# A cross-interaction (CIN) kernel: all products in tiles of 32 rows by 64 columns, without joined leftovers

## The chip, the core and the metric

The kernel runs on one core of one Trainium2 chip. The metric is the device time of one execution in microseconds (us); the figure of the kernel before is the median of three runs. The engines are called PE (TensorE, the matrix unit), PEld (its weight loads), DVE (VectorE), ACT (ScalarE), POOL (GpSimd) and SP (SyncE).

## What is computed

`x` holds 1024 batches of 39 fields with 64 elements each. Three layers each combine the last result with the fields, a different weight for every pair; the sums over the elements go through one final row of weights. All is float32.

```python
def _cin_layer(Xk, X0, W, b):
    Wr = W.reshape(O, Hk, Fdim)
    return jnp.einsum('bhe,bfe,ohf->boe', Xk, X0, Wr) + b[None, :, None]
X0 = sparse_embedding            # (1024, 39, 64)
Xk = X0
for W, b in ((W0, b0), (W1, b1), (W2, b2)):      # 64 outputs each
    Xk = _cin_layer(Xk, X0, W, b)
    outs.append(Xk.sum(axis=-1))
return jnp.concatenate(outs, axis=-1) @ fc_w.T + fc_b
```

## The kernel before

**The algebra.** Both kernels use the same one. The third layer's outputs are only ever summed with weights, so its weights are folded with those of the final row into one matrix `v2`, and that into the weights of layer 2. What is left are two bilinear forms of the fields with 64 outputs each: one is the first layer, the other the folded rest. For each batch and element the two results are multiplied with each other and summed over the elements. A bilinear form is a weighted sum over pairs of fields, and x_a x_b is x_b x_a, so 780 products, each with the sum of two weights, and 39 linear terms (a product with a row of ones) do for both forms. The table of all weights, one row for each output of both forms, is `both`.

**Products and matmuls.** A column is one batch and element, and a block `n` is 2048 columns (32 batches), so there are 32 blocks. GpSimd gathers five operand tiles of 128 rows by 2048 columns for a block (`roll`, L178, an indirect DMA each, L174) from a DRAM table `xd` in which every field is a row; the row numbers stand in `lists`. Six products of two such tiles (`PAIRS`, `product`, L213 and L219, on DVE) hold nearly all pairs. Each is multiplied with its weights `wa` (`multiply`, L555): four matmuls of 128 rows by 128 columns by 512 (L559), the 128 outputs being both forms. A block has 24 such matmuls.

**The leftover.** 32 rows of pairs and 32 of linear terms do not fill a tile. They are done for two blocks at once, with four row tiles of 32: `u` and `v` are gathered as 128 rows by 1024 (`roll_small`, L183), multiplied (L221), and `join` (L567) runs 16 matmuls of 32 rows by 64 columns (L579) and 8 linear ones (L590) into the eight banks of the two blocks.

**Order.** The program is written out in order by hand. `steps` lists the products; DVE makes each four steps ahead (`AHEAD`), into one of four buffers `p`. `finish` (L613) reads a block's four PSUM banks: ACT adds a bias to one form (`z`, L607), DVE multiplies it with the other (`g`, L609) and sums over elements (L620); `fields` (L598) adds the 39 field rows as further rows of `g`. The eight PSUM banks hold two blocks. The operand tiles have two buffers, `rt[0]` and `rt[1]`: when the last product of block `n` is issued, POOL is given the gathers of block `n+2`. The tables `xd` are loaded one block at a time, later by SP.

**Start and end.** `x`'s first two quarters come by ACT's queue into half tables `xh` and are gathered from there. Weights are folded by matmuls (L406 to L487), put into `both` (last copy L503), summed to pairs for one product at a time (`weight_rows`, L515, on DVE at L526), turned by PE (`weight_turn`, L536, L543) and copied to `wa` by ACT (L544). The first three products are made in pieces, and the other weights are turned between the first matmuls. At the end the last block is finished one bank at a time (`finish_quarter`, L627, sums at L631), then `last_weights` (L638) turns the folded row to a column (L640, L649), and a few short matmuls (L745, L757) make the output.

Of the kernel before, what the change touches and what calls it, by code (L numbers as in the profile page):

```python
# [1 line left out]

# [14 lines left out]
NG = 3  # L64
K = NG * F
NX = 128 - K
NT = 5
STEP = (0, 2, 2, 3, 1)
BASE = (0, 35, 11, 1, 17)
OFFSET = (0, 1, 3, 2, -1)  # L70
ONLY = 9
PAIRS = ((0, 1), (0, 2), (3, 1), (3, 2), (0, 4), (3, 4))
NPAIR = len(PAIRS)
SQUARE = 32
NCHUNK = NPAIR + 2
MM = 512
SUB = 1024
BLK = 2048
NA = 10
NQ = NA // 2  # L80
NW = 3
NF = F // NW
BB = BLK // E
SB = SUB // E
NBLK = B // BB
NTAB = 3
# [3 lines left out]
U_STEPS = ((10, -29), (20, -8), (23, -2), (25, -36), (28, 32))  # L90
V_STEPS = ((0, -3), (20, 6), (25, 33), (28, -35), (31, -39))


def label(i, row):
    if row < K:
        return (row % F + BASE[i] + STEP[i] * (row // F)) % F
    e = row - K
    if i == NT - 1 and e < ONLY:
        return F
    return 3 * e + (e >= ONLY) + (e > ONLY) + OFFSET[i]  # L100


def small_labels(r):
    u = 4 + r + 2 * min(r, 23) + sum(by for at, by in U_STEPS if r >= at)
    return u, u + sum(by for at, by in V_STEPS if r >= at)


def split(labels, taken):

    rows = []  # L110
    for row, ab in enumerate(labels):
        key = tuple(sorted(ab))
        if key not in taken:
            taken.add(key)
            rows.append((row, *ab))
    runs = []
    while rows:
        n = 1
        if len(rows) > 1:
            by = [y - x for x, y in zip(rows[0], rows[1])]  # L120
            kind = (rows[0][1] == rows[0][2], rows[0][2] == F)
            while (
                n < len(rows)
                and by[0] == 1
                and by[1] > 0
                and by[2] == (0 if kind[1] else by[1])
                and [y - x for x, y in zip(rows[n - 1], rows[n])] == by
                and (rows[n][1] == rows[n][2], rows[n][2] == F) == kind
            ):
                n += 1  # L130
        row, p, q = rows[0]
        runs.append((row, n, p, q, by[1] if n > 1 else 1, by[2] if n > 1 else 1))
        rows = rows[n:]
    return runs


_taken = set()
RUNS = [
    split([(label(i, row), label(k, row)) for row in range(128)], _taken) for i, k in PAIRS
]  # L140
RUNS.append(split([small_labels(r) for r in range(SQUARE)], _taken))
RUNS.append(split([(small_labels(r)[0], F) for r in range(SQUARE)], _taken))
assert _taken == {(a, b) for a in range(F) for b in range(a, FT)}
assert max(2 * s + b for s, b in zip(STEP, BASE)) <= F
# [3 lines left out]
def cin_kernel(ctx: ExitStack, tc: tile.TileContext, x, w0t, b0, w1, b1, w2, b2, fc_w, fc_b, out):  # L148
# [6 lines left out]
    prods = ctx.enter_context(tc.tile_pool(name="prods", bufs=4))  # L155
    psum = ctx.enter_context(tc.tile_pool(name="psum", bufs=8, space=PSUM))
# [3 lines left out]
    xd = [dram.tile([2 * FT, BLK], F32, name=f"xd{k}") for k in range(NTAB)]  # L160
    xh = [dram.tile([F, SUB], F32, name=f"xh{k}") for k in range(2)]

    def bank(name):
        return psum.tile([128, MM], F32, name=name, tag="po")

    def load(n, engine=nc.sync):
        first = n % 2 * FT
        engine.dma_start(  # L168
            xd[n // 2 % NTAB][first : first + F].rearrange("f (b e) -> f b e", e=E),
            xv[:, n * BB : (n + 1) * BB, :],  # L170
        )
# [53 lines left out]
    with prep as prep:  # L225
# [222 lines left out]
        for k in range(7):  # L448
            turn_w0(k)
# [356 lines left out]
```

## Time and profile before

| what | value |
|---|---|
| time, median of 3 runs | 733.13 us (733.05 to 733.62) |
| span of the profiled execution | 731.4 us |
| matmul and weight-load records, each | 2375 |
| granted TensorE clock (row PEclk) | 9 in all 40 slices, 90% of full speed or more |
| data moved by DMA | 197.24 MB, 270 GB/s on average |
| packets of the gathers' queue (q0) | 65.5% of 16 engines' span |

The profile is one execution. Its span runs from the first to the last instruction; the measured time has a little on top of it. "Busy" is the time in which an engine works on an instruction. A row of the groups gives busy time and the mean of one in ns, then the idle time ahead of the group and what ended it. Rows of a timeline or of the chain begin with the start in us and the duration. `r` stands for the operand tiles, `p` for products, `po` for the banks of sums.

### The profile page before, as it was taken

Reading aid. Unit: us, or ns where it says so; the run is one execution under the profiler, and the core shown is the slowest. Engines: PE = TensorE matmul, PEld = TensorE weight load, DVE = VectorE, ACT = ScalarE, POOL = GpSimd, SP = SyncE. Lnnn points to the kernel's source line nnn. Section 1 sums busy time; section 2 is a strip of 40 time slices with the busy share of each in tenths; the row PEclk is TensorE's granted clock in tenths of the full one; section 3 lists DMA queues with packets and bytes.
Section 4 is the critical chain, followed back from the end, with each engine's and each line's share of the span. In section 5 each row is a group of like instructions: output and inputs, shape, how many; then the busy total and the mean of one; then the engine's idle time right before and its main releaser. Section 6 shows DMA issues by size and latency. Waiting matters only on the chain.

```text
span 731.4 us, 6351 instructions
## 1 busy us (share of the span) xinstructions
PE 724.7 (99%) x2375; PEld 316.1 (43%) x2375; DVE 638.3 (87%) x521; ACT 166.9 (23%) x240; POOL 397.6 (54%) x254
## 2 busy tenths in 40 slices
PE   8999999999999999999999999999999999999998
PEld 4444444444444444444444444444444444444443
DVE  6999798988889988889988889888898988889885
ACT  3332121222212222221222212222121221212222
POOL 6789886536555445754537555455654547545300
PEclk9999999999999999999999999999999999999999
DMA  8997899789575887757679675896767777565700
GB/s 268 376 337 280 315 342 356 290 307 338 232 273 231 281 336 286 270 225 285 269 288 330 223 289 219 304 348 236 268 256 274 301 287 266 224 252 236 288 0 0
DMA packets 65983, 197.24 MB, mean 270 GB/s; under 512 B 40110, under 2 KB 40179, under 8 KB 45984
## 3 DMA queue, kind: packets, MB, share of 16 engines
q0 software_dynamic: 28784, 185.56, 65.5%
q1 hardware_dynamic: 35468, 9.29, 5.5%
q10 hardware_dynamic: 1700, 1.99, 1.0%
q8 instruction: 18, 0.29, 0.1%
q14 instruction: 13, 0.11, 0.0%
HBM read 196.76 MB, written 10.60 MB: 284 GB/s over the span
## 4 chain that ended last, share of the span: by engine, by line
PE 99%; DVE 0%; DMA 0%; issue 0%; ACT 0%; DVEq 0%
PE po L559 91%; PE po L579 4%; PE po L590 2%; PE idle L279 0%; PE pv L406 0%; PE pt L487 0%; PE small L323 0%; PE pv L487 0%; PE pw L418 0%; DMA fcrow<-in_fc_w 0%; PE tr L543 0%; DVE g L609 0%; DVE pairs L526 0%; DVE sums L631 0%; ACT z L607 0%
## 5 line engine op out<-in xcount | busy, mean ns | idle before, releaser
L559 PE MATMUL po<-p,wa 128*128 128x512 f32 x1536 | 666.0, 594 | 0.0
L219 DVE TENSOR_TENSOR p<-r 128x2048 f32<-128x2048 f32 (+2 forms) x198 | 434.1, 2224 | 72.4 <-PE po L559 67.1
L559 PEld LDWEIGHTS po<-p,wa 128*128 128x128 f32 x1536 | 290.5, 190 | 371.7 <-issue 354.6
L174 POOL DMA_INDIRECT r<-xd,lists x156 | 302.3, 1938 | 267.1 <-issue 266.2
L607 ACT ACTIVATE z<-po,columns 64x512 f32<-64x512 f32 x128 | 87.3, 682 | 380.1 <-PE po L590 217.9
L609 DVE SCALAR_TENSOR_TENSOR g<-po,b0s,z 64x512 f32<-64x512 f32 x128 | 95.9, 749 | 9.3 <-ACT z L607 5.3
L602 ACT COPY g<-r 39x1024 f32<-39x1024 f32 x64 | 66.7, 1043 | 155.0 <-DVE sums L620 126.8
L620 DVE TENSOR_REDUCE sums<-g 103x16 f32<-103x1024 f32 x62 | 75.6, 1220 | 2.1
L174 POOL DMA_INDIRECT u<-xd,lists x16 | 38.9, 2432 | 7.5 <-issue 4.6
L174 POOL DMA_INDIRECT v<-xd,lists x16 | 38.5, 2403 | 4.9 <-issue 4.9
L579 PE MATMUL po<-p,wa 32*64 32x512 f32 x512 | 31.6, 600 | 0.0
L221 DVE TENSOR_TENSOR p<-u,v 128x1024 f32<-128x1024 f32 x16 | 19.5, 1218 | 0.0
L579 PEld LDWEIGHTS po<-p,wa 32*64 32x64 f32 x512 | 9.4, 131 | 20.2 <-issue 19.4
L590 PE MATMUL po<-u,wa 32*64 32x512 f32 x256 | 17.0, 587 | 0.0
L174 POOL DMA_INDIRECT r<-xh,lists x8 | 8.0, 996 | 4.8 <-DVE tmp L387 2.7
L590 PEld LDWEIGHTS po<-u,wa 32*64 32x64 f32 x256 | 5.7, 132 | 8.0 <-issue 8.0
L526 DVE TENSOR_TENSOR pairs<-both 128x2 f32<-128x2 f32 (+27 forms) x59 | 6.1, 171 | 0.2
L544 ACT COPY wa<-tr 128x128 f32<-128x128 f32 x8 | 2.1, 266 | 16.2 <-PE tr L543 16.2
L279 PE MATMUL idle<-const-float32-1.0 128*128 128x256 f32 (+1 forms) x8 | 4.0, 596 | 0.8 <-PEq L793 0.8
L543 PE MATMUL tr<-unit,pairs 128*128 128x128 f32 x8 | 2.4, 294 | 2.2 <-DVE pairs L526 2.2
L543 PEld LDWEIGHTS tr<-unit,pairs 128*128 128x128 f32 x8 | 1.2, 151 | 4.7 <-ACT pairs L524 2.7
L168 POOL DMA_DIRECT2D xd<-in_x x3 | 3.2, 1055 | 0.0
(97 smaller groups left out, 56.7 us busy)
## 6 DMA issues: line engine op xcount, KB each, us to landing
xd<-in_x SPq DMA_DIRECT2D x28, 312.0 KB
r<-xd,lists POOLq DMA_INDIRECT x156, 8.9
xd<-in_x POOLq DMA_DIRECT2D x3, 312.0 KB, 7.6
w2s<-in_w ACTq DMA_DIRECT2D x1, 624.0 KB
w1s<-in_w ACTq DMA_DIRECT2D x1, 624.0 KB
w0s<-in_w0t ACTq DMA_DIRECT2D x1, 380.2 KB
xh<-in_x ACTq DMA_DIRECT2D x2, 156.0 KB
xd<-xh SPq DMA_DIRECT2D x2, 156.0 KB
```

The costliest lines, as they stand in the source:

```text
L174: nc.gpsimd.indirect_dma_start(dst, None, table, bass.IndirectOffsetOnAxis(ap=lists[:, k : k + 1], axis=0))
L219: nc.vector.tensor_tensor(p[:, cols], r[:, i, cols], r[:, k, cols], ALU.mult)
L221: nc.vector.tensor_tensor(p[:, 0:SUB], ut[n // 2 % 2], vt[n // 2 % 2], ALU.mult)
L279: nc.tensor.matmul(idle[:, 0:cols], nc.const_aps.tensor(1.0, (128, 128), F32), nc.const_aps.tensor(1.0, (128, cols), F32), start=True, sto ...
L526: nc.vector.tensor_tensor(out, diagonal(a, b, sa, sb), diagonal(b, a, sb, sa), ALU.add)
L559: nc.tensor.matmul(po[n][m], wa[:, c, side : side + 2 * H], p[:, bass.ts(m, MM)], start=n % 2 == 0 and c == 0, stop=n % 2 == 1 and c == NP ...
L579: nc.tensor.matmul(dst[half * H : half * H + H], wa[rows, NPAIR, at : at + H], p[rows, bass.ts(side, MM)], start=t >= 2, stop=t < 2 and ha ...
L590: nc.tensor.matmul(dst[half : half + H], wa[rows, NPAIR + 1, H : 2 * H], ut[n // 2 % 2][rows, bass.ts(side, MM)], start=False, stop=t < 2,)
L602: nc.scalar.copy(gt[H : H + F], rt[n % 2][0:F, 0, bass.ts(m, SUB)])
L607: nc.scalar.activation(z[one], po[n][m][other], AF.Identity, bias=fc0s[other])
L609: return lambda: nc.vector.scalar_tensor_tensor(g[n][m // 2][0:H, at], po[n][m][one], b0s[one], z[one], ALU.add, ALU.mult)
L620: nc.vector.tensor_reduce(sums[:, b_at : b_at + SB], g[n][m // 2].rearrange("p (b e) -> p b e", e=E), AX.X, ALU.add,)
```

## The change

The division of the work is new; the arithmetic in total is not.

**Layout.** The array is always used as four row tiles of 32 rows, and each row tile has its own columns. A super block is 4096 columns (64 batches): row tile `r` of an operand tile holds 1024 of them. A block is 512 of these per row tile, again 2048 columns in all; there are 33 blocks, since the last is cut into two of 256 per row tile. An operand tile ("slot") is 32 fields for each row tile, and there are 14: eight are the fields in turn from a start (`SHIFT`), one is `LEFT` and five are for the remaining seven fields. All are gathered as 128 rows by 1024 columns from the table seen as (field, row tile) rows. The first 4096 columns are gathered in two halves of 512 (`roll_half`), each from a half table `xh` of 32 batches.

**Products.** One slot times five others is one DVE instruction with five results of 512 columns (`product`, L131, L137), so 25 products are five instructions a block. They go into a ring of four such groups. Each product is multiplied in 32x64 matmuls (L471): two forms times four row tiles, each row tile into its own bank (`po`, four banks, two buffers). The two forms go to the two column halves of the array and alternate between blocks. The linear term needs no product: one more set of four matmuls reads slot 1 itself. Nothing is left over, and `join`, `u` and `v` are gone.

**Weights.** `main_pairs` makes the sums for twenty of the products at once; `repeat` copies them to the four row tiles. Twelve chunks are turned (L438) before the first product's matmul, fourteen after eight units (`LAST_TURNS`), a unit being the eight small matmuls of one product. Scratch space of the weights now lies in `rt[1]`, so the gathers of the second super block come after that point.

**Finish and end.** Two banks are finished together: per block two ACT passes, two products and two sums on DVE, and eight field copies on ACT. The last sums are made for 512 columns of two banks. `last_weights` begins with two DVE copies to `kw`.

GpSimd's queue from the first gathers on, before; `xh_71` and `xh_72` are the half tables, `xd_68` the first table, `r_84` and `r_85` the two buffers of operand tiles, `ones` the row of ones:

```order
L369 DMA xd_68<-ones 16x2x128
L174 DMA r_84<-xh_71,lists 128x1024 x4
L174 DMA r_84<-xh_72,lists 128x1024 x2
L168 DMA xd_68<-in_x 1248x1x64
L174 DMA r_84<-xh_72,lists 128x1024 x2
L174 DMA r_84<-xd_68,lists 128x2048
L174 DMA u_86<-xd_68,lists 128x1024
L174 DMA v_88<-xd_68,lists 128x1024
L174 DMA r_85<-xd_68,lists 128x2048 x5
L477 DMA b0s<-in_b 64x1 x2
```

The same place after; `r_82` and `r_83` are now the two buffers of slots, `xh_68` and `xh_69` the half tables, `xd_66` the table of the second super block:

```order
L265 DMA xh_68<-ones 16x128
L81 DMA r_82<-xh_68,lists 128x512 x14
L265 DMA xh_69<-ones 16x128
L75 DMA xd_66<-in_x 2496x1x64
L265 DMA xd_66<-ones 16x256
L81 DMA r_82<-xh_69,lists 128x512 x14
L345 DMA b0s<-in_b 64x1 x2
L346 DMA b1s<-in_b 128x1x1
L347 DMA b2s<-in_b 64x1
L348 DMA fcb<-in_fc_b 96x1
L265 DMA xd_67<-ones 16x256
L265 DMA xd_65<-ones 16x256
```

Before, eleven gathers fill the first 2048 columns and their leftover and five the next block. Now 14 gathers fill the first 2048 columns and 14 the next, and behind the seven smaller DMAs at the end of these rows 14 follow for the next 4096.

DVE's queue where the first products are made, before; `p` is a product, `pairs` the weight sums:

```order
L219 TENSOR_TENSOR p<-r_84 128x512
L526 TENSOR_TENSOR pairs<-both 128x28
L526 TENSOR_TENSOR pairs<-both 128x11
L526 TENSOR_TENSOR pairs<-both 128x26
L526 TENSOR_TENSOR pairs<-both 128x13
L526 TENSOR_TENSOR pairs<-both 128x24
L526 TENSOR_TENSOR pairs<-both 128x15
L526 TENSOR_TENSOR pairs<-both 128x9
L526 TENSOR_TENSOR pairs<-both 128x2
L219 TENSOR_TENSOR p<-r_84 128x512 x3
```

And after; `ring` is the ring of products, and the weight sums now lie in `r_83`:

```order
L431 COPY r_83<-r_83 128x5x96
L137 TENSOR_TENSOR ring<-r_82 128x512 x5
L137 TENSOR_TENSOR ring<-r_82 128x1024
L137 TENSOR_TENSOR ring<-r_82 128x1536
L390 TENSOR_TENSOR r_83<-r_83 128x21
L390 TENSOR_TENSOR r_83<-r_83 128x28 x4
L431 COPY r_83<-r_83 128x6x96
L137 TENSOR_TENSOR ring<-r_82 128x1024
L137 TENSOR_TENSOR ring<-r_82 128x1536
L137 TENSOR_TENSOR ring<-r_82 128x1024
L137 TENSOR_TENSOR ring<-r_82 128x1536
L137 TENSOR_TENSOR ring<-r_82 128x2560 x5
```

Weight sums stood between single products; now five products and a group of five, in two pieces, come first, then five sums and a copy, and after them products in a row. The diff, cut to its core:

```diff
-NT = 5
...
-PAIRS = ((0, 1), (0, 2), (3, 1), (3, 2), (0, 4), (3, 4))
-NPAIR = len(PAIRS)
-SQUARE = 32
...
+NR = 4
+Q = 128 // NR
...
-SUB = 1024
-BLK = 2048
+SUB = 2 * MM
+BLK = NR * MM
+SUP = NR * SUB
+BB = BLK // E
+SB = SUP // E
+MB = MM // E
+NSUP = B // SB
+NTAB = 3
...
+NB = 5
+SHIFT = (3, 7, 11, 15, 19, 0, 1, 2)
+BACK = (5, 6, 7, 0)
+REST = F - Q
+LEFT = len(SHIFT)
+RIGHT = LEFT + 1
+NSLOT = RIGHT + NB
+NPROD = NB * NB
+LINEAR = NPROD
+NCHUNK = NPROD + 1
+DIRECT = 1
+GROUPS = (3, 0, 1, 2, 4)
+ORDER = [NB * k + j for k in GROUPS for j in range(NB)]
+RING = 4
+PB = FT + NR - 1
+LOW, HIGH = 5, 4
+SPLIT = Q - 1
+BLOCKS = [(s, lo, MM) for s in range(NSUP) for lo in (0, MM)]
+BLOCKS[-1:] = [(NSUP - 1, lo, MM // 2) for lo in (MM, MM + MM // 2)]
...
-    def roll(n, tiles=range(NT)):
-        for i in tiles:
-            k = n % 2 * NT + i
-            gather_rows(rt[n % 2][:, i], xd[n // 2 % NTAB][: FT if k < NT else 2 * FT], k)
-
-    def roll_small(n):
-        table = xd[n // 2 % NTAB].rearrange("f (t c) -> (f t) c", c=SUB)
-        for k, dst in enumerate((ut, vt)):
-            gather_rows(dst[n // 2 % 2], table, 2 * NT + k)
-
-    wa = const.tile([128, NCHUNK, 3 * H], F32, name="wa")
+    def roll(s):
+        table = xd[s % NTAB].rearrange("f (r c) -> (f r) c", c=SUB)
+        for k in range(NSLOT):
+            gather(rt[s % 2][:, k], table, k)
+
+    def roll_half(w, slots):
+        table = xh[w].rearrange("f (r c) -> (f r) c", c=MM)
+        for k in slots:
+            gather(rt[0][:, k, bass.ts(w, MM)], table, k)
...
-    rt = [const.tile([128, NT, BLK], F32, name=f"r{k}") for k in range(2)]
-    ut = [const.tile([128, SUB], F32, name=f"u{k}") for k in range(2)]
-    vt = [const.tile([128, SUB], F32, name=f"v{k}") for k in range(2)]
...
+    rt = [const.tile([128, NSLOT, SUB], F32, name=f"r{k}") for k in range(2)]
+    ring = const.tile([128, RING * NB, MM], F32, name="ring")
...
+    def product(n, group, lo=0, hi=NB):
+        s, first, cols = BLOCKS[n]
+        k = GROUPS[group]
+        at = (n * NB + group) % RING * NB
+        r = rt[s % 2][:, :, first : first + cols]
+        one, many = (BACK[k], 0) if k < len(BACK) else (LEFT, RIGHT)
+        nc.vector.tensor_tensor(
+            ring[:, at + lo : at + hi, 0:cols],
+            r[:, one].unsqueeze(1).to_broadcast([128, hi - lo, cols]),
+            r[:, many + lo : many + hi],
+            ALU.mult,
+        )
...
-                xh[k].rearrange("f (b e) -> b f e", e=E), x[k * SB : (k + 1) * SB]
+                xh[k][0:F].rearrange("f (b e) -> b f e", e=E), x[k * BB : (k + 1) * BB]
...
-        for k, cols in enumerate(halves):
-            for i in range(4):
-                gather_rows(rt[0][:, i, cols], xh[k], i)
-                if k and i == 1:
-                    load(1, nc.gpsimd)
-        for k in (1, 0):
-            nc.sync.dma_start(xd[0][0:F, halves[k]], xh[k])
-        roll(0, (4,))
...
+        roll_half(0, range(NSLOT))
+        fill_ones(xh[1], nc.gpsimd)
+        load(1, nc.gpsimd)
+        fill_ones(xd[1], nc.gpsimd)
+        roll_half(1, range(NSLOT))
...
+    def main_pairs(j):
...
+        add_pairs(out[:, 0:n, 0:wrap], 0, b, (1, 0, n), (1, 1, wrap))
+        if wrap < Q:
+            add_pairs(out[:, 0:n, wrap:], wrap, 0, (1, 0, n), (1, 1, Q - wrap))
...
+    def repeat(copy, lo, hi):
+        copy(
+            pairs[:, lo:hi, 1:],
+            pairs[:, lo:hi, 0].unsqueeze(2).to_broadcast([128, hi - lo, NR - 1, Q]),
+        )
...
+    def weight_turn(tr, chunks):
+        for m, c in enumerate(chunks):
+            nc.tensor.transpose(
...
-    def multiply(n, c, p, quarters=range(BLK // MM)):
-        open_block(n)
-        for m in quarters:
-            side = m % 2 * H
...
-    def join(n, p):
-        open_block(n + 1)
...
-        for side in range(2):
-            for t in range(4):
-                for half in range(2):
...
+    def unit_of(n, kind, at):
+        s, first, cols = BLOCKS[n]
+        side = (n % 2 ^ kind) * H
+        order = [*ORDER, LINEAR][: NPROD + kind]
+        c = order[at]
+        if c == LINEAR:
+            src = rt[s % 2][:, DIRECT, first : first + cols]
...
+            src = ring[:, (n * NPROD + at) % (RING * NB), 0:cols]
+
+        def tile_of(r):
+            rows = slice(r * Q, r * Q + Q)
...
+                po[n][side : side + H, r, 0:cols],
+                wa[rows, c, kind * H : kind * H + H],
+                src[rows],
+                start=at == 0,
+                stop=at == len(order) - 1,
+            )
+
+        return tile_of
...
-    def finish_quarter(n, m):
...
     def finish(n):
...
+        s, first, cols = BLOCKS[n]
+        one, other = (slice(k, k + H) for k in ((0, H) if n % 2 == 0 else (H, 0)))
+        for m in range(NR // 2):
+            pair = slice(2 * m, 2 * m + 2)
+            z = work.tile([128, 2, MM], F32, name="z", tag="z")
+            nc.scalar.activation(
+                z[one, :, 0:cols], po[n][other, pair, 0:cols], AF.Identity, bias=fc0s[other]
+            )
...
+        nc.vector.tensor_copy(kw[:, 0 : SPLIT], v2v[:, 1, 0, 1:])
+        at = Q + SPLIT - SHIFT[HIGH]
+        nc.vector.tensor_copy(kw[:, at : at + F - SPLIT], v2v[:, 0, 0, 0 : F - SPLIT])
+        nc.tensor.matmul(pk[H:128, 0:1], kw, b1s, start=True, stop=True)
...
+    FIRST = 12
+    LAST_TURNS = 8
+    for j in range(NB):
+        main_pairs(j)
+    repeat(nc.vector.tensor_copy, 3 * NB, 4 * NB)
+    for k in range(3):
+        repeat(nc.scalar.copy, k * NB, k * NB + NB)
+    for m in range(FIRST // NR):
+        weight_turn(late[:, m], ORDER[m * NR : m * NR + NR])
...
+    for j in range(NB):
+        product(0, 0, j, j + 1)
+    wrap_table()
+    for group in range(1, RING):
+        product(0, group, 0, 2)
+        product(0, group, 2, NB)
+        if group == 1:
+            for j in range(NB):
+                rest_pairs(j)
+            linear_pairs()
+            repeat(nc.vector.tensor_copy, 4 * NB, NCHUNK)
+
+    sides = [[], []]
+    for n in range(len(BLOCKS)):
+        for kind in range(2):
+            sides[n % 2 ^ kind] += [(n, kind, at) for at in range(NPROD + kind)]
+    steps = [[u for u in pair if u] for pair in zip_longest(*sides)]
...
+        if t == LAST_TURNS:
+            rest = [*ORDER[FIRST:], LINEAR]
+            for m in range(0, len(rest), NR):
+                weight_turn(late[:, m // NR], rest[m : m + NR])
+            roll(1)
+            load(2, nc.gpsimd)
+        units = [unit_of(*u) for u in pair]
+        for r in range(NR):
+            for tile_of in units:
+                tile_of(r)
+        for n in [n for n in ends if ends[n] == t]:
+            finish(n)
+        for q in [q for q in reads if reads[q] == t]:
+            if q + RING < len(BLOCKS) * NB:
+                product((q + RING) // NB, (q + RING) % NB)
+            if q % NB == 1:
+                fields(q // NB)
+        for n in [n for n in ends if ends[n] == t]:
+            s, first, cols = BLOCKS[n]
+            if first == MM and s + 2 < NSUP:
+                roll(s + 2)
+                if s + 3 < NSUP:
+                    load(s + 3)
```

585 lines of the change are left out of this document (203 added, 382 removed).

## The prediction

> **What bounds the kernel now.** I read the page's busy shares first, then the chain of work that ended last, then the groups by line and form.
>
> ```profile
> span 731.4 us, 6351 instructions
> PE 724.7 (99%) x2375; PEld 316.1 (43%) x2375; DVE 638.3 (87%) x521; ACT 166.9 (23%) x240; POOL 397.6 (54%) x254
> 17.34 1.82 PE po L559 x2
> 40.30 1.90 PE po L579 x32
> 42.20 0.86 PE po L590 x16
> 43.06 41.40 PE po L559 x96
> ...
> 705.43 20.81 PE po L559 x48
> 726.27 0.69 ACT z L607
> 726.98 0.77 DVE g L609
> 727.77 0.70 DVE sums L631
> ```
>
> PE is busy from 17.34 to 726.24 and the chain never leaves it there. A matmul of the program stands as two records: 96 records in 41.40 us are 48 matmuls of 128x512 at 0.8625 us. The row at 42.20 is the important one: eight matmuls of 32 rows by 64 columns (16 records) take 0.86 us together, as long as one full matmul, so small tiles on different rows and columns of the array run side by side at full worth. The join at 40.30 is two such eights and takes 1.90; 0.18 us of that is left over for entering and leaving the tiled form. From 40.30 on all is back to back. Before that, 24 matmuls and the waits between them take 22.96 us where 20.7 would do.
>
> **What PE does after.** Per 2048 elements before: 24 full matmuls and half of 24 small ones, 24 + 24/2/8 = 25.5 units of 0.86. After: 25 products times two weight halves times four row tiles, and four linear tiles, 204 small matmuls, again 204/8 = 25.5 units. There is nothing to gain in the arithmetic itself: 32 blocks times 25.5 are 816 units either way; the two half-wide blocks at the end leave one over, 816.5. At 0.86 that is 702.2 us, at 0.8625 704.2. I take 702.2, since that row is the same pattern. Gone are the sixteen joins' leftovers, 16 x 0.18 = 2.9 us. New are 14 weight transposes after the eighth unit.
>
> ```profile
> 8.98 1.56 PE pw L418 x7
> L543 PE MATMUL tr<-unit,pairs 128*128 128x128 f32 x8 | 2.4, 294 | 2.2 <-DVE pairs L526 2.2
> L544 ACT COPY wa<-tr 128x128 f32<-128x128 f32 x8 | 2.1, 266 | 16.2 <-PE tr L543 16.2
> 14.84 0.45 DVE L503 COPY both<-flat 64x288 f32<-64x288 f32 x1
> L219 DVE TENSOR_TENSOR p<-r 128x2048 f32<-128x2048 f32 x188 | 424.4, 2289 | 71.6 <-PE po L559 67.1 <-DMA r<-xd,lists 4.3
> L219 DVE TENSOR_TENSOR p<-r 128x1024 f32<-128x1024 f32 x6 | 7.2, 1218 | 0.8 <-DMA r<-xh,lists 0.7
> L219 DVE TENSOR_TENSOR p<-r 128x512 f32<-128x512 f32 x4 | 2.6, 680 | 0.0
> ```
>
> Seven transposes in a row took 1.56, so 0.22 each; at full clock half of that. The 14 cost 1.5 to 3.1 us and I take 1.8.
>
> **The front.** The weight table `both` is complete at 15.3 before. The first half table is twice as large now and stands ahead of `w0s` and `w1s` in ACT's queue, 0.5 us more: 15.8. A product costs 0.15 us and 1.046 ns an element ((2289-1218)/1024); by this the eight sums of `main_pairs`, 608 elements, cost 1.8 and the repeat of 480 elements 0.65. Four transposes 0.9 and one copy of 512 columns 0.7 give 19.9; but eight more transposes stand ahead of the first product in PE's queue, which gives 20.9 at 0.22 each. The first matmul of a product starts at 20.0 to 21.3; I take 20.8, against 17.34 before.
>
> **DVE.** Per block five products of 2560 elements at 0.15 + 2.68 = 2.83, so 14.1 us, and some 5 for finishing, against 25.5 x 0.86 = 21.9 on PE. It still has slack, and the ring lets it run four groups ahead. ACT, 23% busy, gets more and smaller copies for the field rows, and the gathers move 7.3 MB per 4096 elements (14 of half a MB) where they moved 11.5: neither is on the path, and I cost both at nothing.
>
> **GpSimd, where I expect the change to lose.** A gather costs the same whatever the width of its rows, and it does not get on while products follow each other without a gap.
>
> ```profile
> L174 POOL DMA_INDIRECT r<-xd,lists x156 | 302.3, 1938 | 267.1 <-issue 266.2 <-DVE g L609 0.9
> L174 POOL DMA_INDIRECT u<-xd,lists x16 | 38.9, 2432 | 7.5 <-issue 4.6
> ...
> 8.53 0.94 POOL L174 DMA_INDIRECT r<-xh,lists  x1 [0.31 <-issue]
> 9.78 0.94 POOL L174 DMA_INDIRECT r<-xh,lists  x1 [0.30 <-issue]
> 14.45 1.06 POOL L168 DMA_DIRECT2D xd<-in_x  x1
> 39.31 0.65 POOL L479 DMA_DIRECT2D b2s<-in_b  x1
> 51.80 12.45 POOL L174 DMA_INDIRECT u<-xd,lists  x1 [0.30 <-issue]
> 52.35 11.09 DVE L219 TENSOR_TENSOR p<-r 128x2048 f32<-128x2048 f32 x5
> 63.89 2.29 DVE L219 TENSOR_TENSOR p<-r 128x2048 f32<-128x2048 f32 x1 [0.45 <-PE po L559]
> 122.64 2.25 POOL L174 DMA_INDIRECT r<-xd,lists  x1 [0.30 <-issue]
> 125.19 0.94 POOL L174 DMA_INDIRECT r<-xd,lists  x1 [0.30 <-issue]
> 121.78 2.29 DVE L219 TENSOR_TENSOR p<-r 128x2048 f32<-128x2048 f32 x1 [0.27 <-PE po L559]
> 125.22 2.30 DVE L219 TENSOR_TENSOR p<-r 128x2048 f32<-128x2048 f32 x1 [1.14 <-PE po L559]
> ```
>
> Unhindered, a gather takes 0.94 and 0.30 to the next: 1.24 us. The one at 51.80 ends at 64.25, 0.81 after five products in a row end at 63.44 and the first gap, 0.45 us, opens. The one at 122.64 ends at 124.89, again 0.81 after the product that ends at 124.07. So a gather waits for the end of a product that runs and of those that follow it directly.
>
> Here the Trainium skill speaks against the reading on which my sum rests: "SBUF — State Buffer", Who interferes with whom, says that `tensor_tensor` with both inputs in SBUF holds up GpSimd's reads, but infers that it does not hold up the writing of descriptors. By the rule's first half gathers wait as above (the trace agrees, 12.45 against 0.94); by its second they would not, and the start would cost nothing.
>
> Once the pipeline is filled this is bearable: 14 gathers per 4096 elements against 12, in 43.9 us of PE's time, and PE's pace leaves a gap of 4.30 - 2.83 = 1.47 us after every product. At the start it isn't. The first 4096 elements are gathered in two widths of 512, 28 gathers where before there were 16 for the first two blocks, and POOL's queue has them in series:
>
> ```profile
> DMA to landing us min/median/max: 4.6/7.3/7.5
> xd<-ones POOLq DMA_DIRECT2D x1, 16.0 KB, 6.1
> r<-xd,lists POOLq DMA_INDIRECT x156, 8.9
> 40.37 0.64 POOL L369 DMA_DIRECT2D xd<-ones  x1
> ```
>
> The first gather waits for the row of ones, issued near 3.7 and 6.1 on its way: 10 us. Gathers of the half tables landed after 4.6 to 7.5; with half the bytes I take 5.5, and 6.5 for the later ones of half of r's 1 MB.
>
> First stall: slots 0 to 7 are issued by 20. DVE begins products at 18.3 (15.8 + 1.8 + 0.65): 5 x 0.68 + 1.22 + 1.75, then short sums, which let about two gathers through, to 26.2; then 5.9 us of products to 32.1. Slots 10 to 13 come after that, 4 x 1.24 to 37.1, land at 42.6, and the product that needs them ends at 45.4. PE asks for it at 20.8 + 20 x 0.86 + 1.8 = 39.8: 5.6 us.
>
> Second: ones, load, ones (0.64 + 1.06 + 0.64), five gathers (6.2) and one product in their way (2.8) end at 48.4; landed 53.9, product 56.7. PE, resumed at 45.4, asks after five units at 49.7: 7.0 us.
>
> Third: nine gathers, seven small DMAs (5 x 0.65 + 2 x 0.64), five gathers of the next 4096 elements, 21.9 us, and two runs of products in their way, three (8.5) and one (2.8), end at 81.6; landed 88.1, product 90.9. PE asks at 56.7 + 25 x 0.86 = 78.2: 12.7 us.
>
> Together 25 us. If a gather gets on at the end of every product instead of at the end of a row of them, about half of the 26.4 us that products stand in its way (6.4 + 5.9 + 2.8 + 11.3) goes, and the stalls are 12. Upwards, a slower landing (7.3 and 8.9) adds 1.8 + 1.8 + 2.4 = 6: 31. I take 22, near the blocked end, by the row of 12.45. After these, POOL catches up.
>
> **The end.**
>
> ```profile
> 726.16 0.22 PE L640 MATMUL pk<-b1s,v 128*32 128x1 f32 x4
> 726.93 0.15 ACT L649 COPY wfin<-pk 39x1 f32<-39x1 f32 x1
> 727.14 0.63 PE L745 MATMUL py<-sums,wfin 103*32 103x256 f32 x6 [0.24 <-ACT wfin L649]
> ```
>
> Now 5.1 us pass from the last matmul to the span's end, of them 0.69 + 0.77 + 0.70 = 2.2 in finishing a bank. After: one ACT pass of 512 and two each of the DVE steps, 0.69 + 2 x (0.77 + 0.70) = 3.6, so 1.4 more. The last weights' two copies to `kw` stand behind that on DVE, so 0.22, 0.15 and 0.63 above, hidden so far, and some 0.5 of copies and handing over come after it: 1.5 more. Total 8.0.
>
> **The sum.** 20.8 + 702.2 + 1.8 + 22 + 8.0 = 754.8 of span. The profiled execution's span is 731.4 and the median of the three runs 733.1, so 1.7 lies around it: 756.5, told as **756**. The terms' bounds give 744 (12 for the stalls, 20.0 for the front, 1.5 for the transposes, 7.0 for the end) to 771 (31, 21.3, 704.2, 3.1, and two more because the first matmuls after a pause ran at double time, 1.82 for one at 17.34).
>
> **The rivals.** *Gathers keep up.* If reading the list and writing descriptors slip in between or beside these wider, three-dimensional products, POOL needs only 1.24 each: 10 + 28 x 1.24 + 6.9 us of other DMAs + 5 x 1.24 = 57.8, landed 64.3, asked for at 20.8 + 1.8 + 43.9 - 2.83 = 63.7: half a microsecond of stall. The time is 756.5 - 22 = 734.5, and 732.4 with the front at 20.0, the transposes at 1.5 and the end at 7.0: not slower. For it: the short sums at 26 us let gathers through. Against: 12.45. It decides from stalls under some 2 us. Chance 0.25.
>
> *Small matmuls cost by number.* Before, at most 24 small matmuls follow each other; after, 6732 (33 blocks of 204). If the 1.90 of the join is not an entry fee but the steady price, 1.90/16 = 0.119 each, a unit costs 0.95 and 816.5 of them 73 us more: 829; if only the half-wide units don't get cheaper, 51 x 0.43 = 22 more: 778. Against: the 0.86 right behind it. Chance 0.10. The Trainium skill, "TensorE: Matmul & The Clock Gate", Wait — 56ns, not 53.3ns?, gives such a mechanism: without hardware decoding 62 ns per MATMUL, an estimate of 16 x 62 = 0.99 us a unit and 840 us in all. No run here shows a long enough row of small ones to decide it.
>
> **Chances.** 0.65 for the forecast, all of it slower; 0.10 for small matmuls by number, slower; of the 0.25 for gathers that keep up, 0.08 faster by over 0.2% (below 731.7, for which front or end must beat its bound by a microsecond), 0.09 within 0.2%, 0.08 slower. 0.2%, 1.5 us, is about what a measurement of this kernel can tell from no change. Faster 0.08, same 0.09, slower 0.83. The range takes in the forecast's bounds and most of the first rival: 732 to 775; left out are its faster cases and the small matmuls by number.
>
> **What would show it.** Right: PE idle in two or three pieces between 39 and 95 us, ended by DVE products that waited for DMA; gathers of 3 to 12 us beside rows of products; then none. The units at 0.86, and the half-wide ones at 0.43. Wrong: a chain that stays on PE from 21 us on (first rival), or units of 0.9 and more all along (second); or stalls that return every 44 us, which would mean that POOL is the bound in the steady state as well.

## The result and the profile after

The changed kernel takes 751.36 us (median of 4 runs, 750.43 to 752.16), the kernel before 733.09 beside it: a ratio of 1.0242 (1.0221 to 1.0264), 2.4% slower. Forecast were 756 (3.1% slower), in a range of 732 to 775. The direction is right and the size near; the sum behind them isn't right, as its terms show. The page of the changed kernel, its busy engines and its chain:

```profile
span 750.2 us, 28611 instructions
PE 728.7 (97%) x13553; PEld 324.9 (43%) x13553; DVE 613.7 (82%) x361; ACT 244.4 (33%) x366; POOL 397.2 (53%) x277
PE 86%; POOL 4%; DVE 2%; issue 2%; DMA 1%; ACT 0%; DVEq 0%; POOLq 0%; ACTq 0%
```

Its groups of gathers and products:

```profile
L137 DVE TENSOR_TENSOR ring<-r 128x2560 f32<-128x2560 f32 (+4 forms) x172 | 445.5, 2634 | 62.3 <-PE po L471 50.3
L81 POOL DMA_INDIRECT r<-xd,lists x210 | 347.9, 1657 | 262.1 <-PE po L471 194.5
```

A gather takes 1657 ns on average where it took 1938 before, and DVE has more slack (82% busy, before 87%). PE is still the bound, but no longer from 17 us on: GpSimd has 4% of the chain, all of it ahead of 93 us. PE's timeline there, start and duration first:

```profile
21.82 0.66 PE L438 MATMUL late<-unit,r 128*128 128x128 f32 x4 [3.08 <-DVE r L431]
23.52 1.03 PE L438 MATMUL late<-unit,r 128*128 128x128 f32 x4 [1.04 <-ACT wa L450]
25.29 1.12 PE L438 MATMUL late<-unit,r 128*128 128x128 f32 x4 [0.74 <-ACT wa L450]
26.33 9.14 PE L471 MATMUL po<-ring,wa 32*64 32x512 f32 x128
35.41 0.66 PE L438 MATMUL late<-unit,r 128*128 128x128 f32 x4
36.74 0.66 PE L438 MATMUL late<-unit,r 128*128 128x128 f32 x4 [0.68 <-ACT wa L450]
...
39.41 0.44 PE L438 MATMUL late<-unit,r 128*128 128x128 f32 x2 [0.68 <-ACT wa L450]
39.77 15.23 PE L471 MATMUL po<-ring,wa 32*64 32x512 f32 x273
...
72.24 4.55 PE L471 MATMUL po<-ring,wa 32*64 32x512 f32 x80 [0.45 <-DVE ring L137]
...
80.03 15.24 PE L471 MATMUL po<-ring,wa 32*64 32x512 f32 x272 [2.38 <-DVE ring L137]
```

The first product's matmul starts at 26.33, not at 20.8. Between groups of four weight turns PE waits for ACT to copy the group before, in another bank. The first eight units take 9.14, where eight at 0.86 take 6.9: most of that is the clock. The stalls are two, 0.45 and 2.38. The stretches around 26 us (each row has the length, PE's busy time with its records, the granted clock, the busy share of the DMA engines and GB/s):

```profile
24.00:26.00 2.00, 1.26 (x7) 0.50 0.59 160
26.00:28.00 2.00, 2.00 (x18) 0.50 0.60 182
```

And the timeline of the end:

```profile
737.60 0.80 PE L471 MATMUL po<-r,wa 32*64 32x256 f32 x7
738.50 0.68 ACT L511 ACTIVATE z<-po,columns 64x512 f32<-64x512 f32 x1 [5.88 <-PE po L471]
...
739.99 0.69 DVE L518 TENSOR_REDUCE sums<-g 128x8 f32<-128x512 f32 x1
739.99 0.68 ACT L511 ACTIVATE z<-po,columns 64x512 f32<-64x512 f32 x1 [0.81 <-DVE g L515]
740.71 0.74 DVE L515 SCALAR_TENSOR_TENSOR g<-po,b0s,z 64x512 f32<-64x512 f32 x1
741.49 0.69 DVE L518 TENSOR_REDUCE sums<-g 128x8 f32<-128x512 f32 x1
...
742.60 0.34 PE L526 MATMUL end<-b1s,kw 128*64 128x1 f32 x2 [4.20 <-DVE kw L525]
...
744.26 1.07 PE L607 MATMUL end<-sums,wfin 128*32 128x256 f32 x6 [0.51 <-ACT kfin L534]
...
745.98 1.01 PE L618 MATMUL end<-sums,wfin 128*1 128x192 f32 x4 [0.64 <-ACT y L614]
```

The sum, of this execution (752.13, span 750.2): first matmul 26.33; last one ended 738.40, so 11.8 of end; turns 39.77 - 35.41 = 4.4; stalls 2.8; clock 2.0 (9.14 against 7.12 in runs below where it is full: an estimate); what is left of the 712.07 between, 702.9, is the units.

| term | forecast | measured |
|---|---|---|
| first product's matmul | 20.8 | 26.3 |
| units, 816.5 | 702.2 | 702.9, and 2.0 for the clock |
| 14 turns | 1.8 | 4.4 |
| stalls | 22 | 2.8 |
| end | 8.0 | 11.8 |

The stalls are 19 too high, the other terms together nearly 15 too low. So there is a theory to test: **PE came late, and that hid the queue of gathers**, which otherwise would have cost what PE then lost in waiting.

### The profile page after: what moved, and what is told of

The parts are those of the page before. It is cut to its first block, busy times and chain, and to the rows that moved or that the text cites. A ratio compares the mean times of both kernels' runs of the same rounds, so it can differ in the third digit from the quotient of the medians.

```text
span 750.2 us, 28611 instructions
## 1 busy us (share of the span) xinstructions
PE 728.7 (97%) x13553; PEld 324.9 (43%) x13553; DVE 613.7 (82%) x361; ACT 244.4 (33%) x366; POOL 397.2 (53%) x277
## 4 chain that ended last, share of the span: by engine, by line
PE 86%; POOL 4%; DVE 2%; issue 2%; DMA 1%; ACT 0%; DVEq 0%; POOLq 0%; ACTq 0%
PE po L471 86%; POOL r L81 3%; DVE ring L137 1%; DVE g L515 1%; DMA b0s<-in_b 0%; DVE sums L518 0%; ACT z L511 0%; DMA r<-xd,lists 0%; POOL xd L75 0%; PE end L607 0%; PE end L618 0%; POOL xh L265 0%; POOL xd L265 0%; ACT y L614 0%; PE end L530 0%
## 5 line engine op out<-in xcount | busy, mean ns | idle before, releaser
L471 PE MATMUL po<-ring,wa 32*64 32x512 f32 (+1 forms) x13200 | 704.4, 576 | 3.0 <-DVE ring L137 2.8
L137 DVE TENSOR_TENSOR ring<-r 128x2560 f32<-128x2560 f32 (+4 forms) x172 | 445.5, 2634 | 62.3 <-PE po L471 50.3
L81 POOL DMA_INDIRECT r<-xd,lists x210 | 347.9, 1657 | 262.1 <-PE po L471 194.5
L471 PEld LDWEIGHTS po<-ring,wa 32*64 32x64 f32 x13200 | 310.3, 132 | 388.3 <-issue 377.2
L511 ACT ACTIVATE z<-po,columns 64x1024 f32<-64x1024 f32 (+1 forms) x66 | 71.5, 1084 | 458.9 <-PE po L471 388.2
L489 ACT COPY g<-r 32x512 f32<-32x512 f32 (+1 forms) x264 | 159.1, 603 | 10.9 <-DVE sums L518 6.8
L515 DVE SCALAR_TENSOR_TENSOR g<-po,b0s,z 64x1024 f32<-64x1024 f32 (+1 forms) x66 | 82.5, 1250 | 51.9 <-ACT z L511 43.9
L518 DVE TENSOR_REDUCE sums<-g 128x16 f32<-128x1024 f32 (+1 forms) x66 | 78.4, 1188 | 2.3
L81 POOL DMA_INDIRECT r<-xh,lists x28 | 38.7, 1382 | 15.8 <-issue 8.8
L471 PE MATMUL po<-r,wa 32*64 32x512 f32 (+1 forms) x264 | 34.6, 574 | 0.0
L471 PEld LDWEIGHTS po<-r,wa 32*64 32x64 f32 x264 | 11.8, 132 | 7.5 <-issue 7.1
L438 PE MATMUL late<-unit,r 128*128 128x128 f32 x26 | 5.2, 330 | 6.9 <-ACT wa L450 3.8
L438 PEld LDWEIGHTS late<-unit,r 128*128 128x128 f32 x26 | 3.2, 160 | 9.9 <-ACT wa L450 5.2
```

The lines of the kernel that those rows point to most:

```text
L81: nc.gpsimd.indirect_dma_start(dst, None, table, bass.IndirectOffsetOnAxis(ap=lists[:, k : k + 1], axis=0))
L137: nc.vector.tensor_tensor(ring[:, at + lo : at + hi, 0:cols], r[:, one].unsqueeze(1).to_broadcast([128, hi - lo, cols]), r[:, many + lo : ...
L438: nc.tensor.transpose(tr[:, bass.ts(m, 128)], pairs[:, c].rearrange("p r i -> p (r i)"), unit,)
L471: nc.tensor.matmul(po[n][side : side + H, r, 0:cols], wa[rows, c, kind * H : kind * H + H], src[rows], start=at == 0, stop=at == len(order ...
L489: nc.scalar.copy(gt[at : at + Q, u, 0:cols], rt[s % 2][rows, slot, first : first + cols])
L511: nc.scalar.activation(z[one, :, 0:cols], po[n][other, pair, 0:cols], AF.Identity, bias=fc0s[other])
```

## The experiments

**PSUM in tiles of two banks (`two_bank_tiles`).** `early`, `late`, `po` and `end` each become two tiles of two banks; groups of weight turns go to them in turn.

```diff
-    psum = ctx.enter_context(tc.tile_pool(name="psum", bufs=2, space=PSUM))
+    psum = ctx.enter_context(tc.tile_pool(name="psum", bufs=4, space=PSUM))
...
-        return psum.tile([128, NR, MM], F32, name=name, tag="po")
+        return psum.tile([128, 2, MM], F32, name=name, tag="po")
```

> The change as it is, but PSUM is handed out in tiles of two banks instead of four; nothing else is new. In the changed kernel instructions that use different banks of one four-bank tile wait for each other: the weight turns for ACT's copy of the turn before (two waits of 1.04 and 0.74 at 23.5 and 25.3 us, three of 0.68 at 36.7 to 39.4), the transposes into the weight table for all four matmuls, the second pass of a finish for the multiplication of the first (0.81 at the end). Theory A, the tiles cost time but the start is really set by GpSimd's queue of gathers, which the chain shows up to 61 us: the first product's matmul comes near 23 us instead of 26.3, the 14 turns take 2.5 to 3 instead of 4.4, PE then asks for the second block 5 us earlier and its stalls grow from 2.8 to some 8; only the 0.8 at the end is left as a gain, 749 to 751. Theory B, the shared tiles are on the path and the stalls stay near 3: 744 to 746.

750.99 us, ratio 1.0244 (1.0227 to 1.0261). Its PE timeline, and DVE's wait:

```profile
20.42 1.09 PE L438 MATMUL late<-unit,r 128*128 128x128 f32 x8 [2.08 <-DVE r L431]
22.13 0.66 PE L438 MATMUL late<-unit,r 128*128 128x128 f32 x4 [0.61 <-ACT wa L450]
22.72 7.12 PE L471 MATMUL po<-ring,wa 32*64 32x512 f32 x128
29.77 1.09 PE L438 MATMUL late<-unit,r 128*128 128x128 f32 x8
...
71.98 5.87 PE L471 MATMUL po<-ring,wa 32*64 32x512 f32 x80 [6.90 <-DVE ring L137]
```

```profile
64.23 1.28 DVE L514 SCALAR_TENSOR_TENSOR g<-po,b0s,z 64x1024 f32<-64x1024 f32 x1 [8.42 <-DMA b0s<-in_b]
```

Theory A, with the turns a little shorter than it gave: PE starts 3.6 earlier and the turns take 2.2 (29.77 to 31.96, where A had 2.5 to 3), but at 72 us it stands where it stood before, after a stall of 6.9. Behind that the clock is down once more (granted clock 0.5 up to 74.7; 5.87 for the 80 records that took 4.55). DVE there waits for `b0s`, a bias whose load stands behind 28 gathers in GpSimd's queue.

**Small loads issued by SP (`pool_relief`).** Biases and rows of ones leave GpSimd's queue; the gathers and one load of `x` stay.

```diff
-            nc.gpsimd.dma_start(b0s[h : h + H], b0.rearrange("(h o) -> h o", o=1))
+            nc.sync.dma_start(b0s[h : h + H], b0.rearrange("(h o) -> h o", o=1))
```

> The change as it is, but the seven small loads of the biases and rows of ones and the two other rows of ones are issued by SP instead of GpSimd; the gathers and the load of the second super block stay in GpSimd's queue. Theory A (GpSimd's queue sets the start): DVE's wait of 6.9 for b0s goes, the gathers of the second super block start 3.5 to 5 us earlier, and the two stalls of PE (0.45 and 2.38) go: 748 to 749. Theory B (the stalls come from transfers that land late, with DMA at 355 GB/s around 77 us): the stalls stay, 751.

747.71 us, 1.0200 (1.0183 to 1.0217): A. PE waits for no product any more, and the chain has no GpSimd rows. The gathers of the second super block start 10.8 earlier (54.22, in the changed kernel 64.97), where A gave 3.5 to 5. The edit does two things at once, as the first gather too starts earlier (7.07, in the changed kernel 10.80); their shares are not told apart.

**Both (`both_fixes`).** The two edits together.

> Both edits at once: PSUM in tiles of two banks, and the small loads issued by SP. Theory A: the front gains 3 to 4, the 14 turns 1.5 to 2 and the end 0.8, while the shorter queue of GpSimd takes back most of the stalls, so 743 to 746. Theory B (tiles alone matter): the same as two_bank_tiles within 1 us.

741.98 us, 1.0120 (1.0103 to 1.0137), 1 below what A gave. One edit gains 0.4, the other 3.6, both 9.4; by the ratios to the kernel before it is nothing, 3.1 and 8.9, so the 0.4 can't be told from no gain. Each edit uncovers what the other hides. Its timeline (GpSimd's first gather, then PE):

```profile
6.71 1.18 POOL L81 DMA_INDIRECT r<-xh,lists  x1 [3.53 <-DVE unit L269]
```

```profile
23.26 8.52 PE L471 MATMUL po<-ring,wa 32*64 32x512 f32 x128
...
72.83 22.48 PE L471 MATMUL po<-ring,wa 32*64 32x512 f32 x401 [1.76 <-DVE ring L137]
```

The gathers begin at 6.71. In the changed kernel they begin at 10.8, released by the row of ones after a wait of 6.98; issued by SP, it no longer holds them up.

**Plain products at the start (`plain_products`).** For the first four blocks:

```diff
+        if n < 4:
+            for j in range(lo, hi):
+                nc.vector.tensor_tensor(
+                    ring[:, at + j, 0:cols], r[:, one], r[:, many + j], ALU.mult
+                )
+            return
```

> The change as it is, but the products of the first four blocks are issued as five separate instructions of 128x512 with two plain operands, not as one of 128x2560 with a repeated operand; DVE has the slack for it there (0.6 us a group). In the kernel before a gather waited for the whole row of products that followed each other (12.45 and 10.41 us beside five); in the changed one it gets on at the end of every product (2.43 each beside three in a row). Theory A, the form of the instruction decides: gathers of 3.4 us and more appear beside rows of plain products, up to 7 or 10 where two or three groups follow each other, and the stalls grow by 5 to 10: 756 to 762. Theory B, only ends of instructions count: gathers wait at most 0.7 us beyond the 0.94, the stalls shrink, 748 to 751.

746.97 us (two runs), 1.0192 (1.0171 to 1.0212): the stalls are gone, as B has it, and more is gained than it gave. But one gather was held up as A has it. DVE's products and GpSimd's gathers:

```profile
28.16 9.11 DVE L139 TENSOR_TENSOR ring<-r 128x512 f32<-128x512 f32 x15
48.28 9.29 DVE L139 TENSOR_TENSOR ring<-r 128x512 f32<-128x512 f32 x15 [1.66 <-DMA r<-xh,lists]
```

```profile
32.71 5.44 POOL L81 DMA_INDIRECT r<-xh,lists  x1 [1.11 <-issue]
...
50.70 0.94 POOL L81 DMA_INDIRECT r<-xh,lists  x1 [0.30 <-issue]
```

The gather at 32.71 ends 0.88 after fifteen products end at 37.27, eight of which it waited for; beside the fifteen from 48.28 on most go through at 0.94.

**Four edits on both fixes**, each alone. The copies to `kw` moved to the start (`end_early`):

> Both fixes, and the two copies to kw move from the last weights to the start, behind the folded row that they copy. In both_fixes the last sums stand at 734.52, the copies at 734.43 to 734.67, the column matmuls, wfin and kfin until 736.01, and only then the output's matmuls at 736.06. Theory A (the last weights are on the path because their copies stand behind the sums in DVE's queue): the output's matmuls follow the sums at once, 1.5 less, 740.3 to 740.7. Theory B (something else holds the end, the output DMA or the reads of the sums): 741.5 to 742.4.

738.76 us, 1.0083 (1.0065 to 1.0101): A, with 3.2 gained where 1.5 was expected (2.7 by the ratios). The output's matmuls now run ahead of the last sums, but for one of 64 columns, and at full clock (0.63 where both_fixes had 1.05 at 736.06):

```profile
732.46 0.63 PE L606 MATMUL end<-sums,wfin 128*32 128x256 f32 x6 [1.12 <-ACT kfin L533]
...
733.55 0.69 DVE L520 TENSOR_REDUCE sums<-g 128x8 f32<-128x512 f32 x1
```

More empty matmuls (`spin_more`, `spin(4, MM)` for `spin(2, MM)`):

> Both fixes, and four empty matmuls of 512 columns instead of two between the fold and the turns (18.5 to 20.2 us, where PE has 2.3 us without work). In both_fixes the granted clock is 0.5 for 3.4 us around 23 to 27 us, and the first eight units take 8.5 us instead of 6.9. Theory A (the clock falls after the pause of PE): with the pause filled it stays at 1.0, 1.5 less, 740.2 to 740.8. Theory B (it falls at some time after the start anyway): no difference, 741.5 to 742.4. By A a fall may also come later, in another pause: then nothing is gained either.

742.33 us, 1.0126 (1.0096 to 1.0156), and its runs differ by 4.8; the profile is of the longest, 744.47. The first eight units do take 7.12, so the fall of the clock comes from the pause; but PE meets a stall of 3.42 up to 72.61 in place of 1.76, with the clock at 0.72 from 72 to 76 us: A's last sentence. Plain products (`plain_start`):

> Both fixes, and the products of the first four blocks as five plain instructions each, as in plain_products. What is left of PE's stalls in both_fixes is 1.76 at 71 us, behind gathers of 2.4 to 3.5 us. Theory A (a gather waits for the end of the product that runs, and a product of 0.68 lets it in sooner than one of 2.82): the gathers of the second super block come 8 to 10 us sooner and the stall goes: 740.0 to 740.5. Theory B (the stall comes from the landing of the transfers): it stays at 1.5 to 2, 741.5 to 742.5.

740.77 us, 1.0114 (1.0096 to 1.0132): no stall is left (A, a little short), though by the ratios (1.0120 without it) the gain in time is not clear of the noise. The weight matrix ahead of the half table (`w0_first`):

> Both fixes, and the load of the first weight matrix goes ahead of that of the first half table, which is twice as large as in the kernel before. PE waits 1.6 us for this matrix in both_fixes, where the kernel before waits for nothing. Theory A (the load's place in ACT's queue sets the start of the weight table): the wait goes, the first product's matmul comes near 21.7 instead of 23.26; the first gathers come 1 to 2 us later, which costs the stall at 71 us as much again or less: 740 to 742. Theory B (the transfers share the bandwidth whatever their order): the first product's matmul stays near 23, 742 to 743.

743.43 us, 1.0152 (1.0132 to 1.0171), slower than without it and than both theories gave. Its PE timeline:

```profile
21.80 8.50 PE L471 MATMUL po<-ring,wa 32*64 32x512 f32 x128
...
72.81 22.76 PE L471 MATMUL po<-ring,wa 32*64 32x512 f32 x392 [3.22 <-DVE ring L137]
```

The front gains the 1.5 that A gave, and at 72.8 PE stands where both_fixes stood. Once more a front that starts sooner only waits longer. And the longer stall costs more than its length: from 72 to 76 us the mean granted clock is 0.57 here and 1.00 in both_fixes, which is about the 1.5 us by which this run is slower.

**All of them together (`all_in`).**

> Both fixes, the copies to kw early, plain products in the first four blocks, four empty matmuls ahead of the turns, and the first weight matrix loaded ahead of the half table. Theory A (each of them moved the limit to GpSimd's queue, and the plain products give that queue the room): the gains add up, 3.2 at the end, 1.8 for the stall, 1.5 for the front and 1.6 for the clock, from 742.0 to 734 to 735; what is then left against the kernel before is the later first matmul and the longer end. Theory B (the earlier PE runs into the gathers again and its clock falls in the pause): 737 to 739.

734.53 us against 733.49, 1.0012 (0.9997 to 1.0027): not to be told from the kernel before, and A. Its PE timeline:

```profile
21.99 7.12 PE L480 MATMUL po<-ring,wa 32*64 32x512 f32 x128
...
31.23 15.23 PE L480 MATMUL po<-ring,wa 32*64 32x512 f32 x273
...
67.81 22.43 PE L480 MATMUL po<-ring,wa 32*64 32x512 f32 x402
```

PE waits for no product. The kernel before, in the same view, has its first product's matmul here:

```profile
17.14 2.02 PE L559 MATMUL po<-p,wa 128*128 128x512 f32 x2
```

From first to last product matmul 704.9 us pass, where the kernel before takes 709.1: the change's own gain is 4.2. By the prediction's counts the kernel before has 2.9 in the leftovers of its joins and 2.3 in waits among its first 24 matmuls; the 14 turns take back 2.2 (29.04 to 31.23), and most of the rest is the price of a unit (0.8625 before, 0.861 now). The changed kernel starts 4.85 later (21.99 against 17.14; the prediction's 17.34 is the chain's row) and ends 6.1 instead of 5.1 after the last matmul. 4.85 + 1.0 - 4.2 = 1.7, as the spans (733.1 and 731.4) have it.

**Why did gathers wait for whole rows of products before, and not after?** Three runs on the form of the products. The kernel before with one operand repeated (`before_repeat`):

> The kernel before, with one operand of each of the big products read as its first 512 columns four times over, in the three-dimensional form of the changed kernel; its products are not the right ones. Theory A (the repeated operand lets gathers in at the end of every product): no gather takes over 3.4 us, where the kernel before has them up to 12.45 beside rows of products; the time stays within 1 us of the kernel before. Theory B (the form does not matter, the place in the program does): gathers of 7 to 12 us remain in the first 110 us.

The changed kernel with no operand repeated (`two_operands`):

> The change as it is, but both operands of a group are five different slots instead of one repeated five times; its products are not the right ones. Theory A (the repeated operand lets gathers in): gathers of 6 to 12 us appear beside rows of two and more products, PE stalls 5 to 15 us more in the first 100 us, 756 to 766. Theory B (not the repetition, but the width or the number of dimensions): no gather over 3.5 us, 750 to 752.

The kernel before with jumps in all operands (`before_jumps`):

```diff
+            if cols == slice(0, BLK):
+                a = [t.rearrange("p (a b c) -> p b a c", a=2, c=MM) for t in a]
```

> The kernel before, with the big products' 2048 columns taken in quarters 0, 2, 1, 3: the same products, but both operands and the result are read and written with jumps, as the changed kernel's second operand is. Theory A (operands with jumps let a gather in at the end of every product, operands in one piece don't always): no gather over 3.5 us beside rows of products. Theory B (it is not the form of the operands): gathers of 7 to 12 us remain in the first 110 us, as in the run with the repeated operand. By both the time is that of the kernel before within 0.3%.

All three say B on the gathers. With the repeated operand one still takes 14.62 (time 732.83, one run); with jumps (733.82, 1.0015, 0.9992 to 1.0038) the timeline has the same, beside six products in a row:

```profile
55.39 14.64 POOL L174 DMA_INDIRECT u<-xd,lists  x1 [0.30 <-issue]
```

```profile
55.92 13.29 DVE L222 TENSOR_TENSOR p<-r 128x2048 f32<-128x2048 f32 x6
```

and without the repetition, in the changed kernel, each still gets in at the end of one product:

```profile
94.39 16.49 DVE L137 TENSOR_TENSOR ring<-r 128x2560 f32<-128x2560 f32 x6
```

```profile
101.06 2.43 POOL L81 DMA_INDIRECT r<-xd,lists  x1 [0.30 <-issue]
```

That last kernel took 757.61 (one run): its products need more slots before they can start (at 81.03 DVE has waited 10.59 for a gather), and PE stalls for 7.2. So A's time came about, but without A's cause. What decides it stays open; neither the repetition nor the jumps do. The size of a product (2560 elements for 2048) was not varied by itself; with 512 in the changed kernel one gather did wait for eight products, so size remains a candidate that is not shown.

## Why the prediction came out

**The units** were right: 702.9 against 702.2, so 0.861 for eight small matmuls, over 33 blocks on end. The rival of small matmuls by number (778 to 840) is ruled out by that.

**The stalls were the step that failed**: "a gather waits for the end of a product that runs and of those that follow it directly". In the changed kernel none waited for more than one product, and the longest gather took 3.48. Products and gathers from 77 us on:

```profile
77.03 8.32 DVE L137 TENSOR_TENSOR ring<-r 128x2560 f32<-128x2560 f32 x3 [4.84 <-issue]
```

```profile
78.27 2.43 POOL L81 DMA_INDIRECT r<-xd,lists  x1 [0.30 <-issue]
81.00 2.43 POOL L81 DMA_INDIRECT r<-xd,lists  x1 [0.30 <-issue]
83.73 2.43 POOL L81 DMA_INDIRECT r<-xd,lists  x1 [0.30 <-issue]
```

Each ends 0.8 after one product. The kernel before already had rows like this, which the prediction did not look at; here a product follows the first without a gap, and the gather still ends at 88.64, 0.81 after the first product's end at 87.83:

```profile
85.54 4.49 DVE L219 TENSOR_TENSOR p<-r 128x2048 f32<-128x2048 f32 x2 [0.45 <-DMA r<-xd,lists]
86.26 2.38 POOL L174 DMA_INDIRECT r<-xd,lists  x1 [0.30 <-issue]
```

So the rule was read from the row of 12.45 and did not hold for its own trace. One product for each gather is the lower case of the text, 12 of stalls. The rest of the way to 2.8 is, as far as the runs show, PE, which asked up to 10 us later: two_bank_tiles, where it asked earlier, had 8.6. The Trainium skill's "SBUF — State Buffer", Who interferes with whom, infers that such products do not hold up the writing of descriptors. Gathers are held up, 2.43 against 0.94 in this kernel and 12.45 in the one before; whether in reading their list, which by the same section such products do hold up, or in writing descriptors, no run tells. The first rival (gathers keep up) failed too: they kept up only with a late PE.

**The front** was mis-sized by 5.5 and **the turns** by 2.6, mostly for one cause that the text did not have: what shares a four-bank tile waits for each other. Three forms of it show in the timelines: the turns above; the end, where the second `z` at 739.99 waits 0.81 for DVE to read two other banks; and the fold, where a short DVE instruction at 12.15 (at 9.57 with two-bank tiles) waits for matmuls into other banks, and the transposes start when all four matmuls are done:

```profile
12.15 0.23 DVE L332 TENSOR_SCALAR v<-mask,late 128x2 f32<-128x2 f32 x1 [2.51 <-PE late L298]
...
17.05 1.71 DVE L366 STREAM_TRANSPOSE r<-early 128x320 f32<-128x320 f32 x4 [4.67 <-PE early L356]
```

With two-bank tiles the waits shrink or go, the first product's matmul comes 3.6 sooner and the turns take 2.2 instead of 4.4. The chip doesn't ask for them: the Trainium skill's "PSUM — Partial Sum Buffer", PSUM bank collisions raise a hardware error, lets two engines work on different banks at once, and two_bank_tiles agrees. They came from how the program hands out its banks. Another 1.5 of the front is the matrix behind the doubled half table (w0_first); the text had 0.5 for that. The 0.9 that is left is not accounted for.

**The clock** was an upper bound of the text (2) and happened in full (2.0).

**The end**: 11.8 for 8.0. Finishing the banks was right, 3.8 for 3.6 (738.40 to 742.18): the second `z` waits 0.81, but DVE goes on without a gap (739.99 + 0.69, then 740.71), so this wait costs next to nothing. What stands behind it took 8.0 for 4.4. The copies to `kw` were found, but their price was taken as 1.5, with the matmuls behind them at the kernel before's durations. From the sums' end at 742.18 to the output's matmul at 744.26 pass 2.1; these matmuls ran at half clock, 1.07 for what took 0.63; and those at 745.98 wait 0.64 more for ACT to read another bank of the tile `end`. In two_bank_tiles that last wait is gone, and the end is 10.9.

So 756 was near by luck, with the direction right: a start that is later and a longer end do cost what the units don't give back, but the queue of gathers and the late start are two prices of which only the larger is paid, and the forecast added too little of the second to too much of the first.

## What to carry over

When two things hold up the same stage, a start that is late and a queue that fills it, estimate both against the same clock and take the later one, not the sum; an edit to one then gains little alone (0.4, within the noise, and 3.6 here), and both gain more than their sum (9.4). When a layout puts several banks into one tile, look at every pair of engines on that tile for waits that the data doesn't need. Look for rows against a rule in the trace it comes from. And 4.2 us gained between the first and the last matmul can be lost whole to a start that is 4.85 later.

## What was not expected of the hardware

A pause of PE can cost more than its length. Behind one of 3.08 in the changed kernel the granted clock was 0.5 for 6.8 us, and the first eight units took 9.14; behind one of 2.28 in both_fixes it was 0.5 for 3.4 us, and they took 8.52; at full clock they take 7.12. The length alone doesn't decide it: the clock stayed at 1.00 behind the pause of 2.08 in two_bank_tiles, and behind the stall of 2.38 at 77.65 in the changed kernel.

What fits nearly all of it is the idle time within a step. In these traces the granted clock changes only at steps of 3.41 us (at 22.75 and 26.17 in both_fixes, at 23.65 and 30.48 in the changed kernel). It fell behind steps in which PE had been idle for 2.02 us or more (2.02 from 19.34 to 22.75 in both_fixes, 2.62 from 20.24 to 23.65 in the changed kernel) and stayed behind steps with up to 1.89 (68.96 to 72.37 in end_early); the stall of 2.38 was split over two steps, with 1.76 in the longer part. One step doesn't fit: in all_in, from 8.70 to 12.11, 1.70 were enough. No run was made to test this.

A gather beside rows of products ends some 0.8 after a product ends, but not always the first: it waited for five of them in the kernel before (six in its two variants), there in other rows for one; in the changed kernel for one, also without the repeated operand, and, where the products were plain ones of 512 columns, once for eight and once for four (32.71 in plain_products, 93.17 in plain_start).
